# A fused graph, attention and mixture layer: short edge rows, and a written order for the first tokens, weights and products

## The chip, the cores and the metric

The kernel runs on one core of one Trainium2 chip. Its time is the device time in microseconds (us) of one execution; shown is the median of three runs.

## What is computed

One layer of a graph transformer on 625 tokens of 1024 features, all float32. `src` and `dst` hold 20,000 edges, sorted by `dst`.

```python
xn = _layernorm(x)
x = x + gnn(xn, src, dst) + mix(xn)       # both read the same normalised tokens
x = x + ffn(_layernorm(x))
# gnn: two layers h @ W_self + mean @ W_neigh + b, relu between them;
#      mean = segment_sum(h[src], dst) / max(degree, 1)
# mix: q, k, v products, softmax of q over features and of k over tokens,
#      context = k^T v, attn = q context, product with Wo, plus bo
# ffn: softmax router, the best 2 of 8 experts silu(x w1) w2, and a gated shared expert
```

## The kernel before

Every float32 product is made of three TensorE products: each operand is split into a rounded `hi` and the rest `lo`, and `hi*hi + hi*lo + lo*hi` is summed in PSUM. `split` (L93, its instructions stand at L94) makes the pair: ScalarE casts `hi`, and VectorE (or GpSimd, by `eng`) subtracts to get `lo`. Weights come in blocks of 128 x 1024 through `Stream`: `load` issues the transfer on SP's queue (`wraw`, three buffers), `next` splits it into `whi` and `wlo`.

The start of the kernel, which the change touches, runs so:

- `load_x` reads the tokens in five tiles of 128 rows (`xts`); `src` and `dst` come as 10 rows of 2000 (`ei`). All of it is issued on SP: tiles 0 and 1, the edges, the first weight block, tiles 2 to 4.
- `first_stats` and `first_norm` compute mean and inverse deviation (`inv_std`, seven small VectorE instructions and one square root on ScalarE) and normalise. Tiles 0 and 1 are done in one batch, tiles 2 to 4 in another; even tiles are scaled on VectorE (L328), odd ones on ScalarE (L326). `first_turn` transposes a tile on TensorE (`pst`, L276) and splits it into `xnh` and `xnl`.
- The edges are cast to float32 (`edges`, L334), turned by 32 small transposes (`psed`, L338) and one more (`psf`, L343), and copied to `edt` and `first_dst`.
- `keys_step` makes the products of the keys (`psk`, L398 to L400) and then of the self term of the graph layer. There are 64 steps of 12 matmuls; a weight block `o` has two column parts of two steps each. The first three blocks do their columns 0 to 255 first (steps 0 to 5, which need only token tiles 0 and 1), then columns 256 to 625 (steps 6 to 11). `keys_exp` takes a maximum on VectorE (L376) and the exponential on ScalarE (L378), `keys_back` transposes the result (`pskt`, L370). A block `o` is split at a step of block `o-1`; the `lo` parts of blocks 0 to 8 are made on GpSimd (L94 POOL), later ones on VectorE.
- The adjacency is counted by TensorE from one-hot rows: 160 chunks of 125 edges. `one_hots` makes a chunk's pair on VectorE (L454, L455) in a ring `hot` of 40 places, after eight GpSimd instructions (L436 to L446) have prepared `edt`, `srow` and `unit`; `count_chunks` multiplies the pair (`pa`, L477) and adds 16 chunks at a time to `packed` (L481). 36 pairs are made ahead; then each step of the loop makes 4 pairs and counts 4.

A scheduler orders the instructions of an engine by priority and by its own estimates. `keep` (`tc.keep_in_program_order`) pins an instruction behind the one traced before it on its engine, `tc.issue_after` behind a named one, and `tc.high_priority` ranks a block first. [...]After the key stage come queries, values, graph aggregation and experts, on which nothing is changed.

## Time and profile before

| what | value |
|---|---|
| median of 3 runs | 1057.1 us (1052.38 to 1058.31) |
| profiled execution | 1056.29 us, span 1054.3 us |
| mean granted TensorE clock | 0.983 |
| TensorE matmul busy (PE) | 1010.2 us, 96% |
| VectorE busy (DVE) | 601.1 us, 57% |
| ScalarE busy (ACT) | 394.9 us, 37% |
| GpSimd busy (POOL) | 175.0 us, 17% |
| read from and written to memory | 133.06 MB and 30.16 MB, 155 GB/s over the span |

Busy shares are averages over the whole span. PEld is TensorE loading weights beside its matmuls; SPq is the queue on which SP issues transfers. Matmuls overlap, so that the start-to-start distance of two of them, not the duration of one, is their price in a stream. In an answer about waits, a row has the waiting engine with its tile and line, what it waited for, and the total, the number and the longest of the waits. In a timeline, a row has its start, its duration, the engine, the line, the operation, and what the tile is written from.

### The profile page before, as it was taken

Reading aid. Unit: us, or ns where it says so; the run is one execution under the profiler, and the core shown is the slowest. Engines: PE = TensorE matmul, PEld = TensorE weight load, DVE = VectorE, ACT = ScalarE, POOL = GpSimd, SP = SyncE. Lnnn points to the kernel's source line nnn. Section 1 sums busy time; section 2 is a strip of 40 time slices with the busy share of each in tenths; the row PEclk is TensorE's granted clock in tenths of the full one; section 3 lists DMA queues with packets and bytes.
Section 4 is the critical chain, followed back from the end, with each engine's and each line's share of the span. In section 5 each row is a group of like instructions: output and inputs, shape, how many; then the busy total and the mean of one; then the engine's idle time right before and its main releaser. Section 6 shows DMA issues by size and latency. Waiting matters only on the chain. (4 is left out here: it accounts for less than half of the span.)

```text
span 1054.3 us, 14764 instructions
## 1 busy us (share of the span) xinstructions
PE 1010.2 (96%) x5571; PEld 870.8 (83%) x5571; DVE 601.1 (57%) x1190; ACT 394.9 (37%) x577; POOL 175.0 (17%) x206
## 2 busy tenths in 40 slices
PE   6889999999999999999999999999999899999958
PEld 4889998888878888988877999997888688787746
DVE  3899941672343334533337364288776878878632
ACT  3333432232131122222115242175755676677200
POOL 2421002110044100200001004023111213300500
PEclk7999999999999999999999999999999999999979
DMA  6121226665235422322220127477788899879812
GB/s 183 42 80 52 70 81 205 223 217 175 81 110 172 134 76 66 111 72 76 80 81 2 44 78 250 140 221 217 247 261 236 281 306 284 272 256 308 313 50 82
DMA packets 117792, 164.33 MB, mean 156 GB/s; under 512 B 12533, under 2 KB 69885, under 8 KB 117710
## 3 DMA queue, kind: packets, MB, share of 16 engines
q1 hardware_dynamic: 97774, 118.54, 35.9%
q0 software_dynamic: 19936, 44.74, 13.0%
q8 instruction: 47, 0.77, 0.3%
q14 instruction: 35, 0.29, 0.1%
HBM read 133.06 MB, written 30.16 MB: 155 GB/s over the span
## 5 line engine op out<-in xcount | busy, mean ns | idle before, releaser
L94 DVE TENSOR_TENSOR wlo<-wraw,whi 128x1024 fp32r<-128x1024 f32 x140 | 178.7, 1276 | 257.6 <-ACT whi L94 256.5
L94 ACT CAST whi<-wraw 128x1024 fp32r<-128x1024 f32 x149 | 156.4, 1051 | 291.4 <-PE psg L205 66.2
L1120 PE MATMUL pse<-xs,whi 128*128 128x448 f32 (+1 forms) x384 | 109.2, 357 | 0.0
L94 DVE TENSOR_TENSOR wlo<-wmore,whi 128x1024 fp32r<-128x1024 f32 x67 | 86.9, 1297 | 26.3 <-ACT whi L94 25.3
L94 ACT CAST whi<-wmore 128x1024 fp32r<-128x1024 f32 x67 | 70.3, 1049 | 64.3 <-PE psz L205 33.3
L1116 PE MATMUL pse<-xs,wlo 128*128 128x224 f32 (+1 forms) x384 | 90.1, 255 | 0.7 <-DVE wlo L94 0.6
L398 PE MATMUL psk<-xnh,whi 128*128 128x314 f32 (+3 forms) x256 | 82.7, 324 | 0.6 <-ACT xnh L94 0.6
L399 PE MATMUL psk<-xnl,whi 128*128 128x314 f32 (+3 forms) x256 | 79.5, 311 | 1.1 <-DVE xnl L94 1.1
L400 PE MATMUL psk<-xnh,wlo 128*128 128x314 f32 (+3 forms) x256 | 79.5, 311 | 0.0
L1116 PEld LDWEIGHTS pse<-xs,wlo 128*128 128x128 f32 x384 | 72.0, 190 | 2.9 <-DVE wlo L94 2.0
L1172 PE MATMUL psy<-wlo,he 128*128 128x512 f32 (+1 forms) x176 | 69.9, 397 | 3.3 <-DVE wlo L94 2.9
L1120 PEld LDWEIGHTS pse<-xs,whi 128*128 128x128 f32 x384 | 69.0, 189 | 2.4
L1171 PE MATMUL psy<-whi,he 128*128 128x512 f32 (+1 forms) x176 | 69.4, 395 | 0.0
L1173 PE MATMUL psy<-whi,he 128*128 128x512 f32 (+1 forms) x176 | 69.1, 392 | 0.0
L455 DVE TENSOR_SCALAR hot<-iota,srow,unit 125x128 f16<-125x128 f16 x160 | 55.3, 346 | 0.0
L399 PEld LDWEIGHTS psk<-xnl,whi 128*128 128x128 f32 x256 | 49.5, 193 | 1.4 <-DVE xnl L94 1.4
L94 POOL TENSOR_TENSOR xs<-raw,xs 128x512 fp32r<-128x512 f32 (+2 forms) x24 | 34.3, 1452 | 96.7 <-ACT xs L94 75.2
L398 PEld LDWEIGHTS psk<-xnh,whi 128*128 128x128 f32 x256 | 49.3, 193 | 1.1 <-ACT xnh L94 1.1
L400 PEld LDWEIGHTS psk<-xnh,wlo 128*128 128x128 f32 x256 | 49.1, 192 | 0.2 <-POOL wlo L94 0.2
L454 DVE TENSOR_SCALAR hot<-iota,edt 125x128 f16<-125x128 f16 x160 | 45.7, 286 | 1.7 <-POOL edt L444 1.7
L203 PE MATMUL psz<-whi,sth 128*128 128x512 f32 (+1 forms) x80 | 32.1, 401 | 14.4 <-DVE x L1249 12.9
L1172 PEld LDWEIGHTS psy<-wlo,he 128*128 128x128 f32 (+1 forms) x176 | 31.8, 180 | 14.9 <-DVE wlo L94 6.7
(340 smaller groups left out, 2375.1 us busy)
## 6 DMA issues: line engine op xcount, KB each, us to landing
wraw<-in_L_ffn_w_dram SPq DMA_DIRECT2D x65, 512.0 KB, 5.5
wmore<-in_L_ffn_w_dram SPq DMA_DIRECT2D x63, 512.0 KB, 5.2
xsd<-zt POOLq DMA_DIRECT2D x9, 1024.0 KB, 5.6
wraw<-in_L_gnn_W_self_dram SPq DMA_DIRECT2D x16, 512.0 KB, 3.8
wraw<-in_L_gnn_W_neigh_dram SPq DMA_DIRECT2D x16, 512.0 KB, 3.7
wraw<-_ffn_shared_gate_up_dram SPq DMA_DIRECT2D x16, 512.0 KB, 3.8
wraw<-in_L_mix_Wk_dram SPq DMA_DIRECT2D x8, 512.0 KB, 4.2
wraw<-in_L_mix_Wq_dram SPq DMA_DIRECT2D x8, 512.0 KB, 3.7
```

Source lines behind the costliest of these rows:

```text
L94: return (nc.scalar.copy(hi, srcap), (eng or nc.vector).tensor_sub(lo, srcap, hi.bitcast(F32)))
L203: nc.tensor.matmul(acc, xh[:, kt, c], wh[:, k, :], start=f, stop=False)
L398: nc.tensor.matmul(ps[:, :n], wh[:, kt, :], xnh[:, kt, c], start=kt == 0, stop=False)
L399: nc.tensor.matmul(ps[:, :n], wh[:, kt, :], xnl[:, kt, c], start=False, stop=False)
L400: nc.tensor.matmul(ps[:, :n], wl[:, kt, :], xnh[:, kt, c], start=False, stop=kt == KT - 1)
L454: nc.vector.tensor_scalar(h[:ET, :WIN], iota[:ET, :WIN], edst[:, i, g:g + 1], None, op0=ALU.is_equal)
L455: nc.vector.tensor_scalar(h[:ET, WIN:], iota[:ET, :WIN], srow[:ET, i, g:g + 1], unit[:ET, i, g:g + 1].bitcast(F32), op0=ALU.is_equal, op1= ...
L1116: nc.tensor.matmul(ps[a][:, :n], wl[:, k, c], xs[:, kt, 0, :], start=False, stop=False)
L1120: nc.tensor.matmul(ps[a][:, :2 * n], wh[:, k, c], xs[:, kt], start=kt == 0, stop=kt == KT - 1)
L1171: nc.tensor.matmul(acc, h(kt, 0), wh[:, k, :], start=kt == 0, stop=False)
L1172: nc.tensor.matmul(acc, h(kt, 0), wl[:, k, :], start=False, stop=False)
L1173: nc.tensor.matmul(acc, h(kt, 1), wh[:, k, :], start=False, stop=kt == KT - 1)
```

## The change

- The edges are read as 80 rows of 250 (`EP`), issued on ScalarE's queue; `ei` and `edges` move to the pool `edgep`, and four transposes and one take the place of 33. `edt`, `field`, `srow` and `unit` get a new layout of the same size.
- The transfers of tokens 2 to 4 alternate with those of the first three weight blocks on SP.
- Statistics, scales, weight splits, transposes and the first products stand in one written sequence, tile by tile, and nearly all are pinned by `keep`. All five tiles are normalised on ScalarE. Two key steps stand between the transposes of tiles 1 and 2, of 2 and 3, and of 3 and 4, where before four and two stood before tiles 2 and 3.
- Only blocks 0 to 2 have their `lo` part made on GpSimd; blocks 3 to 8 move to VectorE.
- 40 one-hot pairs are made ahead; in the loop the four chunks are counted before new pairs are made, and three pairs a step are made while `ks[0]` is below 40, then four. The register load of a group's first column is queued behind the last pair made.

The diff, without the lines that only follow the new layout in the rarely taken `recount`:

```diff
...
 NG = 10
 ET = 125
 CH = E // (ET * NG)
+EP = E // (2 * ET)
 WIN = 128
 SPAN = NP + WIN
 BITS = 5
...
     def bank(name="ps"):
         return psum.tile([128, 512], F32, name=name, tag="ps")
-    def split(srcap, hi, lo, eng=None):
-        return (nc.scalar.copy(hi, srcap), (eng or nc.vector).tensor_sub(lo, srcap, hi.bitcast(F32)))
+    def split(srcap, hi, lo, eng=None, order=lambda ins: ins):
+        return (order(nc.scalar.copy(hi, srcap)), order((eng or nc.vector).tensor_sub(lo, srcap, hi.bitcast(F32))))
     class Stream:
...
                 self.raw[self.loaded] = r
                 self.loaded += 1
-        def next(self, eng=None):
+        def next(self, eng=None, **order):
             if self.ready:
                 return self.ready.pop(0)
             i = self.used
...
             else:
                 hi = wts.tile([128, D], F32R, name="whi", tag="whi")
                 lo = wts.tile([128, D], F32R, name="wlo", tag="wlo")
-            split(r, hi, lo, eng)
+            split(r, hi, lo, eng, **order)
             b = ap.shape[2]
             return (hi.rearrange("p (a b) -> p a b", b=b), lo.rearrange("p (a b) -> p a b", b=b))
...
         for h in range(2):
             if half is None:
                 order(nc.vector.bn_stats(st6[:mv.shape[0], h, :], xt[:, h * 512:(h + 1) * 512]))
-        nc.vector.bn_aggr(mv, st6[:mv.shape[0]])
-    def inv_std(var, y, z, a):
-        nc.vector.tensor_scalar(a, var, EPS, None, op0=ALU.add)
-        nc.scalar.activation(y, a, AF.Sqrt)
-        nc.vector.reciprocal(y, y)
-        nc.vector.tensor_mul(z, y, y)
-        nc.vector.tensor_mul(z, z, a)
-        nc.vector.tensor_scalar(z, z, -0.5, 1.5, op0=ALU.mult, op1=ALU.add)
-        nc.vector.tensor_mul(y, y, z)
+        (order or (lambda ins: ins))(nc.vector.bn_aggr(mv, st6[:mv.shape[0]]))
+    def inv_std(var, y, z, a, order=lambda ins: ins):
+        order(nc.vector.tensor_scalar(a, var, EPS, None, op0=ALU.add))
+        order(nc.scalar.activation(y, a, AF.Sqrt))
+        order(nc.vector.reciprocal(y, y))
+        order(nc.vector.tensor_mul(z, y, y))
+        order(nc.vector.tensor_mul(z, z, a))
+        order(nc.vector.tensor_scalar(z, z, -0.5, 1.5, op0=ALU.mult, op1=ALU.add))
+        order(nc.vector.tensor_mul(y, y, z))
     def normalise(eng, yt, xt, mean, y, z):
         if eng is nc.vector:
...
         return nat.rearrange("p (c k) -> p k c", k=KT)
-    def to_t(nat, t, hi, lo, order=None):
+    def to_t(nat, t, hi, lo, order=None, both={}):
         for g in range(2):
             ps = bank("pst").rearrange("p (a b) -> p a b", b=128)
             for k in range(4):
...
                 tr = nc.tensor.transpose(ps[:, k, rows(t)], nat[:, kt], ident[rows(t), rows(t)])
                 if order:
                     order(tr)
-            done = split(ps[:, :, rows(t)], hi[:, 4 * g:4 * g + 4, cols(t)], lo[:, 4 * g:4 * g + 4, cols(t)])
+            done = split(ps[:, :, rows(t)], hi[:, 4 * g:4 * g + 4, cols(t)], lo[:, 4 * g:4 * g + 4, cols(t)],
+                         **both)
         return done
     def pad(*tiles):
...
     xnh, xnl = slot_t("xnh"), slot_t("xnl")
     pad(xnh, xnl)
-    ei = big.tile([128, 2, CH * ET], I32, name="ei", tag="big")
+    ei = edgep.tile([EP, 2, 2 * ET], I32, name="ei")
     xts = big.tile([128, NT, D], F32, name="xts", tag="big")
     keep = tc.keep_in_program_order
...
         for r, p in pieces(t):
             keep(nc.sync.dma_start(xts[p, t, :], x[r, :]))
-    for t in range(2):
-        load_x(t)
+    load_x(0)
+    load_x(1)
     for i, e in enumerate((src, dst)):
-        keep(nc.sync.dma_start(ei[:NG, i, :], e.rearrange("(p c) -> p c", p=NG)))
-    st.load(1)
+        keep(nc.scalar.dma_start(ei[:, i, :], e.rearrange("(p c) -> p c", p=EP)))
     for t in range(2, NT):
+        st.load(t - 1)
         load_x(t)
     lnv = const.tile([128, NT, 2], F32, name="lnv")
...
     def first_stats(t):
         stats(xts[rows(t), t, :], lnv[rows(t), t, :], order=keep)
-    def first_norm(a, b):
-        inv_std(lnv[:T, a:b, 1], lnt[:T, 0, a:b], lnt[:T, 1, a:b], lnt[:T, 2, a:b])
-        y, z = lnt[:T, 0, :], lnt[:T, 1, :]
-        nc.vector.scalar_tensor_tensor(z[:, a:b], lnv[:T, a:b, 0], -1.0, y[:, a:b], op0=ALU.mult, op1=ALU.mult)
-        for t in range(a, b):
-            p = rows(t)
-            xt = xts[p, t, :]
-            if t % 2:
-                nc.scalar.activation(xt, xt, AF.Identity, bias=z[p, t:t + 1], scale=y[p, t:t + 1])
-            else:
-                nc.vector.tensor_scalar(xt, xt, lnv[p, t, 0:1], y[p, t:t + 1], op0=ALU.subtract, op1=ALU.mult)
-    def first_turn(t, order=None):
-        return to_t(xts[rows(t), t, :].rearrange("p (k c) -> p k c", c=128), t, xnh, xnl, order)
-    edges = big.tile([128, 2, CH * ET], F32, name="edges", tag="big")
-    nc.scalar.copy(edges[:NG], ei[:NG])
-    edt = edgep.tile([128, 2 * CH, NG], F32, name="edt")
-    pse = bank("psed")[:, :2 * CH * NG].rearrange("p (a b) -> p a b", b=NG)
-    for i in range(2 * CH):
-        nc.tensor.transpose(pse[:ET, i, :], edges[:NG, i // CH, (i % CH) * ET:(i % CH + 1) * ET], ident[:NG, :NG])
-    nc.scalar.copy(edt[:ET], pse[:ET])
-    esrc, edst = edt[:ET, :CH, :], edt[:ET, CH:, :]
-    psf = bank("psf")
-    nc.tensor.transpose(psf[:, :NG], edges[:NG, 1, 0:1].to_broadcast([NG, 128]), ident[:NG, :NG])
+    def first_scale(t):
+        inv_std(lnv[:T, t:t + 1, 1], *(lnt[:T, i, t:t + 1] for i in range(3)), order=keep)
+        keep(nc.vector.scalar_tensor_tensor(lnt[:T, 1, t:t + 1], lnv[:T, t:t + 1, 0], -1.0, lnt[:T, 0, t:t + 1],
+                                            op0=ALU.mult, op1=ALU.mult))
+    def first_norm(t):
+        p = rows(t)
+        keep(nc.scalar.activation(xts[p, t, :], xts[p, t, :], AF.Identity,
+                                  bias=lnt[p, 1, t:t + 1], scale=lnt[p, 0, t:t + 1]))
+    def first_turn(t):
+        return to_t(xts[rows(t), t, :].rearrange("p (k c) -> p k c", c=128), t, xnh, xnl, keep, dict(order=keep))
+    edges = edgep.tile([EP, 2, 2 * ET], F32, name="edges")
+    edt = edgep.tile([128, 2, 2, NG, CH // 2], F32, name="edt")
+    esrc, edst = edt[:ET, 0], edt[:ET, 1]
     first_dst = edgep.tile([128, NG], F32, name="first_dst")
-    nc.scalar.copy(first_dst, psf[:, :NG])
     first_col = edgep.tile([1, NG], I32, name="first_col")
-    with tc.high_priority():
-        for t in range(2):
-            first_stats(t)
-        first_norm(0, 2)
-        first_stats(2)
-        for t in range(2):
-            first_turn(t)
+    def turn_edges():
+        pse = bank("psed")[:, :4 * EP].rearrange("p (a b) -> p a b", b=EP)
+        for i in range(4):
+            nc.tensor.transpose(pse[:ET, i, :], edges[:, i // 2, (i % 2) * ET:(i % 2 + 1) * ET], ident[:EP, :EP])
+        keep(nc.scalar.copy(edt[:ET].rearrange("p a h g j -> p (a h) (g j)"), pse[:ET]))
+        psf = bank("psf")
+        nc.tensor.transpose(psf[:, :EP], edges[:, 1, 0:1].to_broadcast([EP, 128]), ident[:EP, :EP])
+        keep(nc.scalar.copy(first_dst, psf[:, :EP].rearrange("p (g j) -> p g j", g=NG)[:, :, 0]))
     shared = big.tile([128, 8 * NP], F32, name="shared", tag="big")
     kbuf = shared[:, 5 * NP:].rearrange("p (i s) -> p i s", s=NP)
...
         o, i, h = s // 4, s // 2 % 2, s % 2
         if s < 12:
             o, i = s // 2 % 3, s // 6
-        if s in (0, 2, 4):
-            wks[o] = st.next(nc.gpsimd)
         if (o, i, h) == (1, 1, 0):
-            wks[3] = st.next(nc.gpsimd)
+            wks[3] = st.next()
         if i == 0 and h == 0 and 2 < o < 2 * KT - 1:
-            wks[o + 1] = st.next(nc.gpsimd if o < KT else None)
+            wks[o + 1] = st.next()
         if h == 0:
             kps[0] = bank("psk")
         wh, wl = wks[o]
...
             if k < 8 * KT:
                 keys_step(k)
+    def keys_weights(o):
+        wks[o] = st.next(nc.gpsimd, order=keep)
     with tc.high_priority():
-        keys_steps(4)
+        first_stats(0)
+        first_scale(0)
+        first_norm(0)
+        keep(nc.scalar.copy(edges, ei))
+        first_stats(1)
+        first_scale(1)
+        keys_weights(0)
+        first_norm(1)
+        first_stats(2)
+        first_turn(0)
+        first_turn(1)
+        turn_edges()
+        keys_weights(1)
+        first_scale(2)
+        first_norm(2)
         first_stats(3)
+        first_scale(3)
+        keys_weights(2)
+        first_norm(3)
+        keys_steps(2)
+        first_turn(2)
         first_stats(4)
-        first_norm(2, NT)
-        first_turn(2, keep)
+        first_scale(4)
+        first_norm(4)
         keys_steps(2)
-        first_turn(3, keep)
-        last = first_turn(4, keep)
-    field = edgep.tile([128, CH, NG], F32, name="field")
-    srow = edgep.tile([128, CH, NG], F32, name="srow")
-    unit = edgep.tile([128, CH, NG], I32, name="unit")
+        first_turn(3)
+        keys_steps(2)
+        last = first_turn(4)
+    field = edgep.tile([128, 2, NG, CH // 2], F32, name="field")
+    srow = edgep.tile([128, 2, NG, CH // 2], F32, name="srow")
+    unit = edgep.tile([128, 2, NG, CH // 2], I32, name="unit")
     keep(nc.gpsimd.tensor_scalar(field[:ET], esrc, 1.0 / T, -0.496, op0=ALU.mult, op1=ALU.add))
     keep(nc.gpsimd.tensor_scalar(field[:ET], field[:ET], MAGIC, None, op0=ALU.add))
     keep(nc.gpsimd.tensor_scalar(field[:ET], field[:ET], MAGIC, None, op0=ALU.subtract))
...
     keep(nc.gpsimd.tensor_scalar(unit[:ET], field[:ET], BITS * 2.0 ** 23, (127.0 - 2 * BITS) * 2.0 ** 23,
                                  op0=ALU.mult, op1=ALU.add))
-    keep(nc.gpsimd.tensor_sub(edst, edst, first_dst[:ET, None, :].to_broadcast([ET, CH, NG])))
+    keep(nc.gpsimd.tensor_sub(edst, edst, first_dst[:ET, None, :, None].to_broadcast([ET, 2, NG, CH // 2])))
     keep(nc.gpsimd.tensor_copy(first_col, first_dst[:1]))
...
     nc.gpsimd.memset(packed, 0.0)
     def one_hot(h, i, g):
-        nc.vector.tensor_scalar(h[:ET, :WIN], iota[:ET, :WIN], edst[:, i, g:g + 1], None, op0=ALU.is_equal)
-        nc.vector.tensor_scalar(h[:ET, WIN:], iota[:ET, :WIN], srow[:ET, i, g:g + 1],
-                                unit[:ET, i, g:g + 1].bitcast(F32), op0=ALU.is_equal, op1=ALU.mult)
-    pa, made, counted = [None], [0], [0]
+        e = (slice(0, ET), i // 8, g, slice(i % 8, i % 8 + 1))
+        nc.vector.tensor_scalar(h[:ET, :WIN], iota[:ET, :WIN], edst[e], None, op0=ALU.is_equal)
+        return nc.vector.tensor_scalar(h[:ET, WIN:], iota[:ET, :WIN], srow[e], unit[e].bitcast(F32),
+                                       op0=ALU.is_equal, op1=ALU.mult)
+    pa, made, counted, hots = [None], [0], [0], []
     def one_hots(n):
         for _ in range(n):
             c = made[0]
             if c < NG * CH:
                 made[0] += 1
-                one_hot(hot[:, c % RING, :], c % CH, c // CH)
+                hots.append(one_hot(hot[:, c % RING, :], c % CH, c // CH))
     def count_chunks(n):
         for _ in range(n):
...
             h = hot[:ET, c % RING, :]
             nc.tensor.matmul(pa[0][:, :WIN], h[:, WIN:], h[:, :WIN], start=i == 0, stop=i == CH - 1)
             if i == CH - 1:
-                first_v = nc.vector.value_load(first_col[0:1, g:g + 1], min_val=0, max_val=N - 1)
+                with tc.issue_after(hots[-1].ins):
+                    first_v = nc.vector.value_load(first_col[0:1, g:g + 1], min_val=0, max_val=N - 1)
                 to = packed[:T, ds(first_v, WIN)]
                 nc.vector.tensor_add(to, to, pa[0][:T, :WIN])
...
     nc.tensor.transpose(psb[:, :KT], b0n, ident[:KT, :KT])
     nc.vector.tensor_copy(b0t, psb[:, :KT])
     with tc.issue_after(last[0].ins), tc.issue_after(last[1].ins):
-        one_hots(RING - 4)
+        one_hots(RING)
     knat = slot_n("knat")
     hself = slot_t("hself", F32)
     while ks[0] < 8 * KT:
         keys_steps(1)
-        one_hots(4)
         count_chunks(4)
+        one_hots(3 if ks[0] < 5 * KT else 4)
     ath = atp.tile([128, NT, XP], F32R, name="ath")
...
```

More of the change, by code (lines that the diff above doesn't have):

```diff
@@ L557, in recount @@
         ct = tmp.tile([128, HW], F32, name="ct", tag="tmp")
-        nc.vector.tensor_tensor(edst, edst, first_dst[:ET, None, :].to_broadcast([ET, CH, NG]), op=ALU.add)
+        nc.vector.tensor_tensor(edst, edst, first_dst[:ET, None, :, None].to_broadcast([ET, 2, NG, CH // 2]), op=ALU.add)
         nc.vector.tensor_scalar(field[:ET], esrc, float(HW), None, op0=ALU.is_ge)
@@ L567, in recount @@
                     h = tmp.tile([128, WIN + HW + 1], F16, name="hrare", tag="tmp")
-                    nc.vector.tensor_scalar(h[:ET, :WIN], iota[:ET, :WIN], edst[:, i, ds(g, 1)], None, op0=ALU.is_equal)
-                    nc.vector.tensor_scalar(h[:ET, WIN:WIN + HW], iota[:ET, :HW], esrc[:, i, ds(g, 1)],
-                                            field[:ET, i, ds(g, 1)], op0=ALU.is_equal, op1=ALU.mult)
+                    nc.vector.tensor_scalar(h[:ET, :WIN], iota[:ET, :WIN], edst[:, i // 8, ds(g, 1), i % 8], None, op0=ALU.is_equal)
+                    nc.vector.tensor_scalar(h[:ET, WIN:WIN + HW], iota[:ET, :HW], esrc[:, i // 8, ds(g, 1), i % 8],
+                                            field[:ET, i // 8, ds(g, 1), i % 8], op0=ALU.is_equal, op1=ALU.mult)
                     nc.tensor.matmul(ps[:, :HW], h[:ET, :WIN], h[:ET, WIN:WIN + HW], start=i == 0, stop=i == CH - 1)
```

## The prediction

> **What bounds the kernel now.** The page comes first: TensorE.
>
> ```profile
> PE 1010.2 (96%) x5571; PEld 870.8 (83%) x5571; DVE 601.1 (57%) x1190; ACT 394.9 (37%) x577; POOL 175.0 (17%) x206
> ...
> PE   6889999999999999999999999999999899999958
> ...
> PEclk7999999999999999999999999999999999999979
> ```
>
> PE is full but for the first three slices (26.4 us each) and the last two. Which idle times those are, PE's answer about waits says, over the whole run:
>
> ```profile
> PE psz L203 <- DVE x L1249: 12.9, 1, 12.9
> PE psed L338 <- ACT edges L334: 7.9, 1, 7.9
> PE pskt L370 <- ACT shared L378: 3.0, 1, 3.0
> ...
> PE pst L276 <- DVE xts L328: 2.0, 1, 2.0
> ```
>
> The 12.9 us lie at 1012, behind a gather that the change leaves alone; the others lie in the first 68 us. The timeline of that stretch:
>
> ```profile
> 11.57 3.51 ACT L334 CAST edges<-ei 10x4000 f32<-10x4000 int32 x1
> ...
> 15.23 6.86 PE L338 MATMUL psed<-ident,edges 10*125 10x10 f32 x32 [7.85 <-ACT edges L334]
> ...
> 22.12 3.28 PE L276 MATMUL pst<-ident,xts 128*128 128x128 f32 x16
> ...
> 25.62 0.38 PE L398 MATMUL psk<-xnh,whi 128*128 128x256 f32 x1 [0.22 <-ACT xnh L94]
> ...
> 34.48 1.38 PE L276 MATMUL pst<-ident,xts 128*128 128x128 f32 x8 [2.04 <-DVE xts L328]
> ...
> 43.72 0.44 PE L399 MATMUL psk<-xnl,whi 128*128 128x370 f32 x1 [0.79 <-DVE xnl L94]
> ```
>
> Tokens 0 and 1 are scaled by 11.7, but PE turns them at 22.12, behind the edges; the first product is at 25.62. PE waits for the scaling of tile 2, and the wide steps run from 43.7. The clock in windows of 2 us (the last three columns are granted clock, DMA share, GB/s):
>
> ```profile
> 32.00:34.00 2.00, 0.44 (x4) 0.24 (x2) 1.67 (x7) 0.47 (x2) 1.75 (x4) 1.00 0.61 182
> ...
> 36.00:38.00 2.00, 2.00 (x11) 2.00 (x10) 1.27 (x5) 0.49 (x1) 0.82 (x3) 0.50 0.02 7
> ```
>
> After a gap of 2.04 us the clock halves. Last, the timeline at the later stall of 3.0 us:
>
> ```profile
> 55.99 4.81 POOL L94 TENSOR_TENSOR wlo<-wraw,whi 128x1024 fp32r<-128x1024 f32 x2 [4.65 <-ACT whi L94]
> ...
> 56.11 2.39 DVE L455 TENSOR_SCALAR hot<-iota,srow,unit 125x128 f16<-125x128 f16 x1
> ...
> 58.42 2.43 DVE L454 TENSOR_SCALAR hot<-iota,edt 125x128 f16<-125x128 f16 x1
> ...
> 65.25 0.78 DVE L376 TENSOR_REDUCE mx<-shared 128x1 f32<-128x625 f32 x1
> ...
> 67.31 0.77 PE L370 MATMUL pskt<-ident,shared 128*128 128x128 f32 x5 [2.98 <-ACT shared L378]
> ```
>
> A one-hot of 0.3 us takes 2.4 while GpSimd subtracts a weight; the maximum L376 stands behind some 40 pairs on DVE, its exponential behind that, and PE behind both.
>
> **The change part by part.** PE is full from 68 us to 1012 and its work there is the same, so the sum is the shift of the transposes L370 that start at 67.31.
>
> *Edges.* The cast of 4000 numbers a row took 3.51 us, 0.88 ns each; 500 make 0.44, and with the 0.17 us of the smallest ACT instructions 0.6. 33 transposes end 6.9 us after the first starts, 0.21 each at half clock; five make 1.1. Transfers: the same 156 KB as 160 rows of 1000 bytes instead of 20 of 8000. SP loses two issues (0.41 and 0.30 us), ScalarE gains them at about 2.5 us, where it is idle until 9.0. The landing of short rows is not shown: between no later than before and 2 us later. I take 0, as the cast waits for `first_norm(0)` at 9.1 anyway; later than that, ScalarE is held with tile 1 behind it.
>
> *Transfers in turn.* SP's order is tokens 0, 1, weight 0, token 2, weight 1, token 3, weight 2, token 4. The bytes are the same (4.2 MB), and in the trace they have landed by about 17.3 us (DMA share 1.15 at 16 to 17, then 0.34). Token 2 stays near 12.3, token 4 moves from about 16 to 17.3. Nothing below needs it before 27. Weight 0 is not timed, only bounded: after token 1 (7.2), before token 2 (12.3). I take 11; at 12.3 all that follows comes 1.2 later.
>
> *Normalising tile by tile.* DVE loses three scalings (0.81 us) and gains three more chains of seven small instructions, 1.4 us each by 8.80 to 10.39; ScalarE gains three of 1.24 us and three roots of 0.2. So I lay the written order out by hand. Tile 0: statistics 4.65 to 6.2, scale 7.8, normalised 9.1, turned on PE by 10.9. Edge cast to 9.6. Tile 1: statistics from 7.85, scale 11.0. ScalarE then has weight 0 (1.05) to 12.05 and tile 1 to 13.3; PE turns it by 15.0; four casts (0.55) to 15.6, DVE's subtractions (0.65) behind the statistics of tile 2 to 16.5. PE turns the edges beside that, and the first product starts at 16.0 instead of 25.62. Steps 0 and 1 (24 matmuls at 0.213 cold, 0.118 warm) end at about 20.
>
> *Behind it.* ScalarE: the two edge copies (0.6), weight 1 to 17.55, root of tile 2. GpSimd's `lo` of weight 1 lasts from 17.6 to 20.0, and the chain of tile 2 has TENSOR_SCALARs; in the trace such a one took 2.12 us beside GpSimd (L252). So tile 2 is normalised at 20.5 to 21.75; tile 3, behind its statistics (1.5), chain and weight 2, at 24.8. The casts of tile 2 (behind tile 3's norm) end at 26.3, its subtractions at 27.0; only then come statistics and chain of tile 4 (1.5 and 2.3, with some 1 us of collisions with the eight GpSimd edge instructions), scaled at 30.8 to 32.05. ScalarE still has casts and key copies of tiles 3 and 4, to 34.9. Step 6 starts at about 34.5 where it did at 41.99.
>
> PE has by then steps 2 to 5 (11.4 us at most), turned tiles 2 and 3, and two gaps, about 2.9 and 1.5 us. Here a rule bears: the Trainium skill, "TensorE: Matmul & The Clock Gate", section "HAM oscillation", asks for no idle gap above about 3.4 us. By that rule these gaps cost nothing further. The row above speaks against it: 2.04 us sufficed, and 3.4 us then ran at half clock. I follow the trace: half of 3.4, 1.7 us. Step 6 starts in effect at 36.2, against 43.3 before (the end of step 11 at 55.55, less 72 matmuls of 0.17). That is 7.1 us.
>
> *The stall L370.* The `lo` parts of blocks 3 to 8 leave GpSimd: six of 2.4 us, each of which held a DVE instruction as long; DVE pays 1.23 us instead (L94 DVE). The Trainium skill, "SBUF — State Buffer", section "Who interferes with whom", speaks against moving them: a DVE instruction with two SBUF inputs contends with a GpSimd one that reads SBUF. But GpSimd has nothing else there, so by rule and trace the price is 1.23. From the last subtraction (35.6) DVE needs 40 pairs at 0.385 (start to start), a maximum 0.93, one `lo` 1.28, the second maximum 0.93, the exponential 1.1: ready at 55.2. PE arrives at 36.2 + 12.3 + 0.5 + four steps of 2.03 = 57.1. No stall: 3.0 us more, with 1.9 to spare. Shift in all 10.1.
>
> *Three pairs a step.* Per block of four steps (8.6 us on PE) DVE has 12 pairs 4.6, `lo` 1.28, maximum 0.93, an addition 0.25: 7.1. The lead shrinks from 40 to about 10 chunks at the 27th step and stays there. Cost 0 while DVE keeps its 1.5 us a block; without that cover PE waits at L477. The register loads (10) and the moved `ei` and `edges` (buffers of `big` come free earlier) have no row: 0, bounded by -0.5 and +1.
>
> Sum: the profiled 1056.29 (span 1054.3 and 2.0 around it) less 10.1 is 1046.2. The median shown is 0.8 above that execution, so I say 1046.
>
> **The rivals.**
> *A smoother start.* The scheduler puts unpinned steps 2 to 5 into the gaps, the clock stays warm, the port is free: step 6 at about 33, the shift then limited by DVE's 55.2 to some 12 to 14 us: 1043. For it: 41 to 44 has three gaps below 0.9 us and a full clock. Against: tile 4's chain ends late whatever PE does.
> *A head of the line.* Everything on ScalarE is pinned; a weight landing 3 us late holds the token behind it. Each such wait passes to tile 4; two cost 5 to 6: 1051. For: 512-byte rows of the weights, three transfers ahead of token 4. Against: all have landed by 17.3.
> *Slower: one-hots become the bound.* With three pairs a step and all `lo` parts on DVE, PE waits at L477 in each block. It decides from a DVE block of 8.6 us, that is pairs of 0.51 us; at the 0.63 us that the page's means of L454 and L455 add up to, a block takes 10.0 and ten blocks lose 14, so 1060. Against: these means hold overlap and port waits, and the start-to-start distance is 0.385.
> *It does not do what it says:* PE's unpinned steps or the edge transposes are ordered as before; then about 3 us remain, 1053.
>
> **How the numbers follow.** Below 0.5% (5.3 us) the measurement cannot tell a gain from no change. Hand sum 0.62 (1046, 1043 to 1049), smoother 0.16, head of the line 0.12 (half of it within 0.5%), order as before 0.06, slower 0.04. Faster 0.85, same 0.11, slower 0.04. The range 1040 to 1052 leaves out the slow case, most of "as before", and the ends of the others.
>
> **What would show it.** Five edge transposes instead of 33; first L398 near 16 (right: below 18); the first step over 370 columns near 34.5, preceded by two gaps and a clock of 0.5; no wait of `pskt` above 1 us; DVE `lo` parts of 1.2 us from block 3 on and no one-hot of 2.4; no wait of L477 for `hot`. I am wrong if the wide steps start after 39, or if PE waits in the key stage for `hot` or `wlo`.

## The result, and the profile after

The changed kernel takes 1041.44 us (median of four runs, 1040.14 to 1043.89), against 1056.19 for the kernel before (four runs, 1052.38 to 1058.31). The ratio is 0.9867, with a 95% interval of 0.9832 to 0.9902. The profiled executions stand at 1041.64 us (span 1039.9) and 1056.29 (span 1054.3).

The page after, in the lines that were shown of before: busy times, TensorE in 40 slices, granted clock.

```profile
PE 1004.7 (97%) x5543; PEld 865.0 (83%) x5543; DVE 594.3 (57%) x1214; ACT 396.7 (38%) x583; POOL 159.0 (15%) x200
...
PE   7999999999999999999999999999999999999878
...
PEclk8999999999999999999999999999999999999989
```

TensorE's work is the same but for 28 small transposes; only the first slices are fuller. What it waits for in the first 170 us, by the answer about waits:

```profile
PE pst L277 <- ACT xts L327: 6.9, 4, 2.2
PE pswarm L240 <- DVE cold L237: 1.5, 1, 1.5
PE pskt L364 <- ACT shared L372: 0.6, 1, 0.6
PE psk L390 <- ACT xnh L95: 0.2, 1, 0.2
```

The 7.9 us for the edges are gone, and 3.0 of `pskt` have become 0.6. In their place stand four waits for tiles that ScalarE has yet to scale (L327). TensorE's timeline, cut to what carries the reading:

```profile
9.42 1.06 PE L277 MATMUL pst<-ident,xts 128*128 128x128 f32 x8 [2.18 <-ACT xts L327]
12.37 1.97 PE L277 MATMUL pst<-ident,xts 128*128 128x128 f32 x8 [1.89 <-ACT xts L327]
14.13 0.97 PE L343 MATMUL psed<-ident,edges 80*125 80x80 f32 x4
...
14.97 0.56 PE L390 MATMUL psk<-xnh,whi 128*128 128x256 f32 x1
...
21.17 1.10 PE L277 MATMUL pst<-ident,xts 128*128 128x128 f32 x8 [1.87 <-ACT xts L327]
...
29.85 0.99 PE L277 MATMUL pst<-ident,xts 113*128 113x113 f32 x8 [0.97 <-ACT xts L327]
31.09 0.78 PE L390 MATMUL psk<-xnh,whi 128*128 128x370 f32 x3 [0.24 <-ACT xnh L95]
...
43.78 0.71 PE L364 MATMUL pskt<-ident,shared 128*128 128x128 f32 x5
```

Three landmarks say where the time came from. The wide steps start at 31.09 instead of 41.99. The first transposes L364, which close them, start at 43.78 instead of 55.55: 11.8 us. The second start at 53.12 instead of 67.31: 14.2 us. At the first query product it is still 14.2 (150.74 for 164.92). From there to the end the two profiles take 889.2 and 889.4 us; in all the profiles below this stretch lies between 886.8 and 892.8, so that the close agreement of these two is partly luck. The spans differ by 14.4.

The chain that now sets the start is on VectorE and ScalarE. VectorE's timeline has one long instruction in it, beside GpSimd's subtraction of weight 1:

```profile
16.66 2.40 POOL L95 TENSOR_TENSOR wlo<-wraw,whi 128x1024 fp32r<-128x1024 f32 x1 [3.39 <-ACT whi L95]
```

```profile
16.91 2.16 DVE L256 TENSOR_TENSOR lnt<-lnt 128x1 f32<-128x1 f32 x1
19.10 0.16 DVE L257 TENSOR_TENSOR lnt<-lnt 128x1 f32<-128x1 f32 x1
```

A product of two columns of one number each takes 2.16 us, where the next one takes 0.16. It ends with GpSimd's subtraction (19.07 and 19.06), and all of tile 2 waits behind it.

### The profile page after: what moved, and what is told of

It is laid out like the page before. It is cut to its first block, busy times and chain, and to the rows that moved or that the text cites. A ratio compares the mean times of both kernels' runs of the same rounds, so it can differ in the third digit from the quotient of the medians.

```text
span 1039.9 us, 14735 instructions
## 1 busy us (share of the span) xinstructions
PE 1004.7 (97%) x5543; PEld 865.0 (83%) x5543; DVE 594.3 (57%) x1214; ACT 396.7 (38%) x583; POOL 159.0 (15%) x200
## 5 line engine op out<-in xcount | busy, mean ns | idle before, releaser
L95 DVE TENSOR_TENSOR wlo<-wraw,whi 128x1024 fp32r<-128x1024 f32 x146 | 185.5, 1270 | 262.1 <-ACT whi L95 258.2
```

Source lines behind the costliest of these rows:

```text
L95: return (order(nc.scalar.copy(hi, srcap)), order((eng or nc.vector).tensor_sub(lo, srcap, hi.bitcast(F32))))
```

## The experiments

For each run three things are compared: the time, the start of the first transposes L364 (55.55 before; 43.78 changed), which measures the first stage, and the start of the first query product (164.9 before; 150.7 changed), where the key stage is over. The landmarks leave out what happens at the end of the kernel, where a gather scatters by some microseconds from run to run. Ratios are to runs of the kernel before on the same chip, and differ clearly only where their intervals part. A landmark comes from one profiled execution; the two of the changed kernel lie 1.1 us apart at both landmarks, so a difference of that size says nothing. "Later" below is against the changed kernel's first profile.

| run | ratio and interval | first L364 | first query product |
|---|---|---|---|
| edges alone | 0.9927 (0.9905 to 0.9949) | 47.24 | 159.7 |
| long edge rows | 0.9932 (0.9910 to 0.9954) | 52.40 | 159.4 |
| lo parts on GpSimd | 0.9918 (0.9891 to 0.9945) | 45.09 | 158.1 |
| key copies pinned | 0.9903 (0.9870 to 0.9936) | 46.93 | 153.9 |
| no pins | 0.9873 (0.9850 to 0.9896) | 46.75 | 153.7 |
| one-hots as before | 0.9861 (0.9834 to 0.9888) | 49.23 | 155.4 |
| tokens first | 0.9853 (0.9826 to 0.9881) | 46.53 | 153.5 |
| scale first, 12 pairs in the loop | 0.9896 (0.9870 to 0.9922) | 50.25 | 156.4 |
| scale first | 0.9831 (0.9808 to 0.9854) | 42.59 | 149.5 |
| gaps filled | 0.9867 (0.9846 to 0.9888) | 43.63 | 150.6 |
| changed kernel again | 0.9845 (0.9824 to 0.9866) | 44.85 | 151.8 |
| scale first, filled, ring of 36 | 0.9807 (0.9779 to 0.9836) | 42.78 | 149.0 |

### The edges alone

The kernel before, with the edges read as 80 short rows, turned by five transposes and laid out as in the change; the rest untouched.

```diff
-        keep(nc.sync.dma_start(ei[:NG, i, :], e.rearrange("(p c) -> p c", p=NG)))
+        keep(nc.scalar.dma_start(ei[:, i, :], e.rearrange("(p c) -> p c", p=EP)))
...
-    for i in range(2 * CH):
-        nc.tensor.transpose(pse[:ET, i, :], edges[:NG, i // CH, (i % CH) * ET:(i % CH + 1) * ET], ident[:NG, :NG])
+    for i in range(4):
+        nc.tensor.transpose(pse[:ET, i, :], edges[:, i // 2, (i % 2) * ET:(i % 2 + 1) * ET], ident[:EP, :EP])
```

> The kernel before with the edges alone changed: 80 short rows issued on ScalarE's queue, five transposes, the new layout; order, weights and one-hots as before. Theory A (the gain is made of three separate parts; the order of ScalarE and VectorE sets where the wide steps start): the transposes of tiles 0 and 1 move from 22.1 to about 15, the first product from 25.6 to about 18 to 19, but tile 2 is still scaled in one batch with tiles 3 and 4, so the wide steps start only 4 to 7 us earlier, and the wait of pskt stays near 3 us: 1050 to 1052. Rival B (short edge rows carry the whole change): wide steps near 32 and 1042 to 1044. Rival C (the edges were off the path): 1056.

1048.74 us, a little better than theory A's 1050 to 1052. Tiles 0 and 1 are turned at 14.07, the wide steps start at 34.48, 7.5 us earlier: more than expected. But 3.0 of the 8.3 us at the first transposes (L371 here) are lost again by the queries. TensorE's waits and windows of this run (each row ends with the granted clock, the DMA share and GB/s):

```profile
PE pskt L371 <- ACT shared L379: 3.4, 1, 3.4
```

```profile
58.00:62.00 4.00, 2.58 (x11) 2.58 (x12) 4.00 (x17) 2.97 (x6) 1.30 (x1) 0.54 0.00 0
62.00:66.00 4.00, 4.00 (x22) 3.81 (x21) 4.00 (x14) 0.00 (x0) 1.15 (x1) 0.60 0.39 116
```

TensorE comes earlier and waits longer for the maximum and exponential behind VectorE's queue (3.4 us for 3.0), and half clock follows this wait. In the changed kernel, where blocks 3 to 8 no longer stand in VectorE's way, the same edges keep what they bring, as the next run shows.

The rest of the change takes the wide steps from 34.48 to 31.09. The written order itself, tile by tile instead of in two batches, was not undone in any run, so its own part in these 3.4 us is not shown.

### The edges undone

```diff
-    ei = edgep.tile([EP, 2, 2 * ET], I32, name="ei")
+    ei = big.tile([128, 2, CH * ET], I32, name="ei", tag="big")[:NG]
...
-        keep(nc.scalar.dma_start(ei[:, i, :], e.rearrange("(p c) -> p c", p=EP)))
+        keep(nc.sync.dma_start(ei[:, i, :], e.rearrange("(p c) -> p c", p=NG)))
```

and the 33 transposes and the old layout with it.

> The changed kernel with the edges as before: 10 rows of 2000 issued on SP behind token tile 1, a cast of 3.5 us, 32 transposes and one; all else as changed, so the cast stands on ScalarE between tile 0 and tile 1. Theory A: ScalarE is held 2.9 us longer ahead of tile 1, and PE 5.8 us longer ahead of the first product; the first product goes from 15.0 to about 23 to 24, the wide steps from 31.5 to about 37 to 39: 1047 to 1049. Rival B (short rows carry everything): 1054 or more. Rival C (the written order hides the edges): within 2 us of 1041.

1049.42 us, just above the expected 1047 to 1049. The cast of 10 rows holds ScalarE from 8.87 to 12.38 with tile 1 behind it, and TensorE turns edges for 6.89 us at half clock before the first product at 23.8; wide steps at 39.70. With ten columns a transpose TensorE counted as busy, and yet its clock did not come up: it is 0.50 in every window from 14 to 26. By difference the short rows are worth 8.6 us in the changed kernel, at the first L364 and at the queries alike, and alone 5.3 at the queries.

### The lo parts back on GpSimd

```diff
-            wks[3] = st.next()
+            wks[3] = st.next(nc.gpsimd)
...
-            wks[o + 1] = st.next()
+            wks[o + 1] = st.next(nc.gpsimd if o < KT else None)
```

> The changed kernel with the lo parts of blocks 3 to 8 made on GpSimd again. Theory A: the wide steps start at 31.5 as in the changed kernel, GpSimd holds VectorE for three times 2.4 us before the second maximum, less the 1.2 us of the block that VectorE no longer makes; the second pskt waits 4 to 7 us instead of 0.6: 1045 to 1048. Rival D (the stall before came from the order of VectorE's queue, not from GpSimd): pskt waits below 1 us, 1041.

1048.17 us, just above theory A's 1045 to 1048. The stall is back, and larger, and with it the one-hots that GpSimd holds; TensorE's wait, and one of them on VectorE's timeline:

```profile
PE pskt L364 <- ACT shared L372: 4.0, 1, 4.0
```

```profile
44.55 2.56 DVE L472 TENSOR_SCALAR hot<-iota,srow,unit 125x128 f16<-125x128 f16 x1
```

The third L364 comes 11.3 us after the second instead of 8.7, since half clock follows this wait too (0.50 at 58 to 62). At the queries 7.4 us are lost, 1.3 of them before the first L364: there the clock fell after a gap of 2.75 us ahead of tile 2, before GpSimd had any of the blocks put back. The lo parts themselves are thus worth about 6. The second maximum stands behind 80 one-hot instructions here, in the changed kernel and in the kernel before, so the rival that blamed the order of VectorE's queue falls.

### The key copies pinned

```diff
-                nc.scalar.copy(kbuf[:, o % 3, c0:c0 + n], ps[:, :n])
+                (keep if s < 6 else lambda ins: ins)(nc.scalar.copy(kbuf[:, o % 3, c0:c0 + n], ps[:, :n]))
```

In the changed kernel ScalarE cast the first half of tile 2 at 22.55, ahead of the scaling of tile 3 at 23.03. Its timeline:

```profile
21.02 0.35 ACT L396 COPY shared<-psk 128x256 f32<-128x256 f32 x1
...
22.55 0.58 ACT L95 CAST xnh<-pst 128x512 fp32r<-128x512 f32 x1
23.03 1.25 ACT L327 ACTIVATE xts<-xts,lnt 128x1024 f32<-128x1024 f32 x1
```

The source has them the other way round, and both are pinned. But a pin holds an instruction behind the one traced just before it, and that was the key copy of step 1, which is not pinned: it went ahead (21.02), and with it the end of the chain of pins.

> The changed kernel with the three key copies among steps 0 to 5 pinned as well, so that ScalarE casts tile 2 behind the scaling of tile 3, and tile 3 behind that of tile 4, as the prediction assumed. Theory A (the prediction's 3 us too late were this order): wide steps at 33 to 35 instead of 31.5, and two gaps on TensorE of which one is above 2 us; 1043 to 1046. Rival E (the order of these casts is hidden by VectorE): wide steps within 0.5 us of 31.5, 1041. On the clock: if a gap above 2 us halves it, 1.7 us come on top.

1045.30 us: in theory A's range, but not by its way. With the copies pinned ScalarE does follow the source, and yet the wide steps start at 31.65, only 0.6 later, as rival E said. (Here tile 1 was turned at full clock, which brought tile 2 forward by 0.9, so the order itself is worth about 1.5, by difference.) The larger loss at the landmark is the clock:

```profile
29.70 0.99 PE L277 MATMUL pst<-ident,xts 113*128 113x113 f32 x8 [1.66 <-ACT xts L327]
31.65 1.29 PE L390 MATMUL psk<-xnh,whi 128*128 128x370 f32 x3 [0.95 <-ACT xnh L95]
```

```profile
32.00:34.00 2.00, 2.00 (x7) 1.56 (x7) 1.07 (x5) 0.03 (x1) 0.00 (x0) 0.50 0.00 0
34.00:36.00 2.00, 2.00 (x8) 2.00 (x7) 2.00 (x12) 0.00 (x0) 0.00 (x0) 0.50 0.00 0
36.00:38.00 2.00, 2.00 (x9) 2.00 (x9) 2.00 (x11) 0.00 (x0) 0.00 (x0) 0.60 0.00 0
```

Gaps of 1.66 and 0.95 us with 1 us of transposes between them were followed by half clock for some 6 us of the wide steps: 46.93 instead of 43.78 at the first L364. This is one execution; the ratio's interval overlaps that of the changed kernel.

### No pins

Statistics, scales, weights, transposes and edge copies written as in the change, without `keep`.

> The changed kernel with the sequence written as it is but nothing in it pinned (statistics, scales, weights, transposes and edge copies left to the scheduler's priorities); transfers pinned as before. Theory A (the order itself, tile by tile, is what counts, and priorities keep most of it): wide steps at 31 to 35, 1041 to 1046. Rival F (only the pins make the order): the edges or the statistics run ahead, wide steps after 37, 1047 or more.

1044.63 us; wide steps at 34.06. The scheduler kept nearly all of the order. What it moved is at the head of ScalarE's queue:

```profile
6.85 0.61 ACT L425 CAST edges<-ei 80x500 f32<-80x500 int32 x1 [4.38 <-DMA ei<-in_dst_dram]
7.36 0.20 ACT L254 ACTIVATE lnt<-lnt 128x1 f32<-128x1 f32 x1
8.87 1.04 ACT L95 CAST whi<-wraw 128x1024 fp32r<-128x1024 f32 x1 [1.30 <-DMA wraw<-in_L_mix_Wk_dram]
9.82 1.24 ACT L330 ACTIVATE xts<-xts,lnt 128x1024 f32<-128x1024 f32 x1
```

The root of tile 0 waits behind edges that land at 6.8, and its scaling behind weight 0, which lands at 8.8: tile 0 is scaled at 9.82 instead of 8.04. In this profile the first of these transposes (L367 here) is 3.0 us later; by the times the two kernels can't be told apart.

### The one-hots undone

```diff
-        one_hots(RING)
+        one_hots(RING - 4)
...
-        count_chunks(4)
-        one_hots(3 if ks[0] < 5 * KT else 4)
+        one_hots(4)
+        count_chunks(4)
```

> The changed kernel with the one-hots as before: 36 pairs ahead, four pairs in each step ahead of the counting. Theory A (three pairs a step cost and bring nothing of their own; VectorE has cover): the second maximum stands behind 36 pairs and none of the loop's first four or behind 40 as before, the wait of pskt stays at 0.6 or up to 1, and later ones stay away: 1041 to 1043. Rival G (three pairs a step give VectorE the time for the lo parts of blocks 4 to 8): with 16 pairs a block VectorE needs 8.6 us a block, as much as TensorE, so pskt or the first product of a block waits in several blocks: 1044 to 1048.

1044.09 us, above theory A's range and at the lower end of rival G's, but by a way that neither had. VectorE's timeline, and TensorE's after it:

```profile
25.13 1.27 DVE L249 BATCH_NORM_STATS2 bnst<-xts 113x6 f32<-113x512 f32 x2
28.92 0.25 DVE L471 TENSOR_SCALAR hot<-iota,edt 125x128 f16<-125x128 f16 x1 [2.52 <-POOL edt L460]
29.09 0.20 DVE L250 BATCH_NORM_AGGREGATE lnv<-bnst 113x2 f32<-113x12 f32 x1
```

```profile
32.53 1.08 PE L277 MATMUL pst<-ident,xts 113*128 113x113 f32 x8 [3.91 <-ACT xts L327]
```

A one-hot stands between the statistics of tile 4 and their aggregate, and waits 2.52 us for GpSimd. VectorE took its queue in order: the statistics end at 26.4, the aggregate starts at 29.09. `issue_after` holds the 36 pairs of the block behind the last subtraction; the first pairs of the loop are not in the block, and four places of the ring are free, so the scheduler let them go ahead. With 40 pinned pairs there is no free place. Tile 4 is 2.7 us late, half clock follows its gap of 3.9 us, and the first L364 is at 49.23, 5.4 us later. After it no product waited for VectorE, in this run or with three pairs a step. The profile is of the slowest of four executions (1047.14, the others 1040.91 to 1044.10), and by the ratios this kernel can't be told from the changed one: the trace shows the way, and the 5.4 us are of this execution. The kernel before shows the same wait in VectorE's timeline, ahead of the subtraction of tile 2 at 37.51:

```profile
36.73 0.26 DVE L454 TENSOR_SCALAR hot<-iota,edt 125x128 f16<-125x128 f16 x1 [1.66 <-POOL edt L444]
```

### Tokens first

```diff
+    st.load(1)
     for t in range(2, NT):
-        st.load(t - 1)
         load_x(t)
+    st.load(3)
```

> The changed kernel with the transfers in the order of before: weight 0 ahead of tokens 2 to 4, weights 1 and 2 behind them. Theory A (all bytes have landed by 18 us and nothing waits for a transfer after token 0): weight 1 lands at 17 instead of before 15.5 and holds ScalarE, whose queue has it ahead of tile 2, by about 1.5 us; wide steps at 32 to 34: 1041 to 1044. Rival H (transfers in turn are the gain): wide steps after 35, 1046.

1043.27 us, in theory A's range, but not by its way. ScalarE waited 0.72 us for weight 1, which landed at 15.48; its cast began no later than in the changed kernel (15.52). Nothing waited for weight 2. The first of these transposes (L365 here) is 2.8 us later. In this run the clock stood at half from about 14 to 28 us; the steps ended late and held ScalarE's key copies, ahead of tile 2's scaling and again at 28.50. Whether the order of the transfers has a part in that isn't shown; by the times it makes no difference that can be measured.

### Scale first, with 12 pairs in the loop

The chain of tile 2 written ahead of weight 1, to be over before GpSimd subtracts it; and 12 of the 40 pairs moved into the loop's first step.

```diff
-        keys_weights(1)
         first_scale(2)
+        keys_weights(1)
...
-        one_hots(RING)
+        one_hots(RING - 12)
...
-        one_hots(3 if ks[0] < 5 * KT else 4)
+        one_hots((3 if ks[0] < 5 * KT else 4) + (12 if counted[0] == 4 else 0))
```

> The changed kernel with two changes of order: the scale of tile 2 is written ahead of weight 1, so that its chain on VectorE is over before GpSimd subtracts weight 1, and 12 of the 40 pairs made ahead are made in the loop's first step, behind the second maximum. Theory A (tile 2's chain, held 2.2 us by GpSimd, sets all that follows; the second maximum stands behind 40 pairs): tile 2 is turned at about 19 instead of 21.2, wide steps at 29 to 30, pskt does not wait: 1038.5 to 1039.5, that is 2 to 3 us less than the changed kernel. Rival I (the transfers or ScalarE's own work set tile 4): wide steps stay at 31, and 0.6 us is all: 1041.

1045.94 us: both theories failed. Twelve pairs were now free to go ahead of tile 4, and did: the first waited 2.51 us for GpSimd and stands at 27.94, ahead of the aggregate of tile 4 at 28.10. TensorE waited 3.7 us for its scaling, and the wide steps started at 33.2 at half clock. (Tile 2 was turned at 19.76, near what theory A said.)

### Scale first alone

> The changed kernel with the scale of tile 2 written ahead of weight 1 and nothing else (all 40 pairs stay pinned behind the last subtraction). Theory A (in the run with 12 pairs in the loop, pairs that were not pinned went ahead of tile 4's chain and cost 3 to 4 us; without them the earlier tile 2 is a gain): tile 2 turned at 19.5 to 20, no hot ahead of tile 4, wide steps at 29 to 30.5, 1038.5 to 1040.5. Rival I (tile 4 is set by something else): wide steps at 31, 1041. Rival J (the clock, not the order, decides: an earlier tile 2 only makes a longer gap elsewhere): wide steps at 30 at half clock, 1042 to 1043.

1039.00 us, as theory A said: tile 2 turned at 19.80, wide steps at 29.90 at full clock, first L364 at 42.59, 1.2 us before the changed kernel's first profile and 2.3 before its second. No pair goes ahead of tile 4, which fits the reading of the run with 12 pairs in the loop and of the one with the one-hots undone. The interval of its ratio overlaps that of the changed kernel, so that a gain in the time is not shown.

### The gaps filled, and the changed kernel again

Matmuls on a zero tile in the gaps, their result not used: 29 instead of 20 at the start, 7 between tiles 0 and 1, 7 behind step 1, 4 behind step 5.

```diff
+    def fill(n):
+        ps = bank("psfill")
+        for i in range(n):
+            keep(nc.tensor.matmul(ps, cold[:, :128], cold, start=i == 0, stop=i == n - 1))
```

> The changed kernel with matmuls on a zero tile in TensorE's gaps: 29 instead of 20 at the start, 7 between the transposes of tiles 0 and 1, 7 behind step 1, 4 behind step 5; their result is not used. Theory K (the clock halves after gaps of 1 to 3 us, at a point that differs from run to run, and that is most of the scatter of these kernels): clock 1.0 from 6 to 40 us, first product still at 15, step 1 over at 18, wide steps at 31; not faster in the profile than the changed kernel's, but the runs lie closer, 1039.5 to 1041. Rival L (the clock is the same in every run of a kernel, and fillers only take time): 1041 to 1043 with the same scatter, wide steps later by up to 1 us.

> The changed kernel once more, unchanged. Theory K: its profile shows the half clock in other windows than the first profile (11.4 to 17.7 there), and its wide steps or the transposes behind step 11 shift by 0 to 4 us with it; times between 1040 and 1045. Rival L: the same windows within 0.5 us, transposes behind step 11 at 43.8.

The changed kernel's second profile is 1.1 us later at the first L364. The clock made that, in the same program. First its windows from 18 to 24, then those of the first profile:

```profile
18.00:20.00 2.00, 0.29 (x3) 0.09 (x1) 1.86 (x6) 0.22 (x1) 0.96 (x1) 1.00 0.00 0
20.00:22.00 2.00, 0.93 (x9) 0.93 (x9) 1.63 (x6) 1.87 (x4) 0.00 (x0) 1.00 0.87 261
22.00:24.00 2.00, 2.00 (x13) 2.00 (x12) 1.33 (x6) 2.00 (x3) 1.38 (x1) 0.60 0.05 9
```

```profile
18.00:20.00 2.00, 1.30 (x11) 1.09 (x10) 1.86 (x6) 0.12 (x1) 1.05 (x1) 1.00 0.00 0
20.00:22.00 2.00, 0.83 (x8) 0.83 (x9) 1.63 (x6) 1.87 (x4) 0.00 (x0) 1.00 0.84 248
22.00:24.00 2.00, 2.00 (x19) 2.00 (x18) 1.42 (x6) 2.00 (x3) 1.28 (x1) 1.00 0.08 22
```

In the second the clock came up two microseconds earlier (full at 16 to 18, 0.56 in the first), so steps 0 and 1 were over sooner, the gap ahead of tile 2 grew from 1.87 to 2.79 us, and the clock fell again. Filled, it is 1.00 in every window from 4 to 44 us; tile 2 is turned at 20.20, but the wide steps start at 30.94, much as in the first profile. So theory K is right that the clock differs from run to run, and wrong on the scatter: the filled runs lie between 1039.84 and 1045.53, with a median of 1041.85. Of the 4.4 us between the spans of the changed kernel's two profiles 1.1 are there at the queries, and 2.6 come from VectorE's last wait for the gather, first profile first:

```profile
1007.91 1.41 DVE L1266 SCALAR_TENSOR_TENSOR x<-ys,top,x 113x512 f32<-113x512 f32 x2 [1.43 <-DMA ys<-ysd,slot]
```

```profile
1012.07 1.41 DVE L1266 SCALAR_TENSOR_TENSOR x<-ys,top,x 113x512 f32<-113x512 f32 x2 [4.07 <-DMA ys<-ysd,slot]
```

### The best version

Scale first; a ring of 36, all pinned; fillers 26, 6 and 3.

> The changed kernel with the scale of tile 2 ahead of weight 1, a ring of 36 pairs of which all 36 are made ahead and pinned, and matmuls on a zero tile in TensorE's gaps (26 at the start, 6 between tiles 0 and 1, 3 behind step 5). Theory A: with a full clock steps 0 and 1 end at 18, tile 2 is turned at 18.2 and tile 4 by 28.5, the wide steps start at 28.5 to 29.5, the second pskt does not wait; the transposes behind step 11 at 41 to 41.5 (43.8 and 44.9 in the two profiles of the changed kernel, 42.6 with the scale alone), the first query product at 147.5 to 148.5 (150.7 and 151.8): 1037.5 to 1039.5. Rival I (tile 4 is set by ScalarE's work): transposes behind step 11 at 42.5 and 1039 to 1040.5.

1040.20 us on a chip where the kernel before took 1060.47: a ratio of 0.9807 (0.9779 to 0.9836), below both of the changed kernel (their intervals reach 0.9832 and 0.9824 at the low end, so they overlap, and a gain is not shown). Steps 0 and 1 end by 18, tile 2 is turned at 18.07, and `pskt` no longer waits. But the wide steps start at 30.09, and the first L364 is at 42.78, no better than with the scale alone. The numbers are rival I's, yet ScalarE is not the cause: it waited 2.04 us for VectorE ahead of the scaling of tile 3. GpSimd's timeline, then VectorE's:

```profile
19.62 2.40 POOL L95 TENSOR_TENSOR wlo<-wraw,whi 128x1024 fp32r<-128x1024 f32 x1 [0.62 <-ACT whi L95]
```

```profile
19.63 2.40 DVE L322 SCALAR_TENSOR_TENSOR lnt<-lnv,lnt 128x1 f32<-128x1 f32 x1
```

The last instruction of tile 3's chain started 0.01 us after GpSimd's subtraction of weight 2 and was held for all of it. The wait was moved from tile 2 to tile 3.

This is decided by hundredths of a microsecond. In the changed kernel the same instruction of tile 3 started at 22.71, 0.01 us before the subtraction, and took 0.16; with the scale alone at 21.52 against 21.53, and took 0.16 too. Other executions of these kernels may fall either way; no run shows how often.

## Why the prediction was right, and where its sum was off

The time lies in the range (1040 to 1052), 4.6 us below the forecast of 1046. What was to be gained and why is right: the edges out of TensorE's way, an earlier tile 2 to 4, and the stall gone with GpSimd's blocks. The sum gave 10.1 us where the profiled executions differ by 14.65: 4.7 more before the first L364 (11.8 for 7.1), 0.6 less at the stall, and the rest behind the key stage. The large misses point the same way, and it is the width of the range that holds the result. By its own rule (0.8 above the profiled execution) the sum gives 1047, not 1046.

- *First product.* Forecast 16.0, measured 14.97. Weight 0 was taken to land at 11; the run without pins shows it at 8.8, and its cast came at 9.79, in time that ScalarE had free. Edges as forecast: cast 0.59 us for 0.6, five transposes 1.1 for 1.1.
- *The chain of tile 2.* The block by GpSimd came as forecast (2.16 us), but on the TENSOR_TENSOR at 16.91, where the working named a TENSOR_SCALAR. The rule that the prediction cites from the Trainium skill ("SBUF — State Buffer", section "Who interferes with whom") on two SBUF inputs covers this one, and the time agrees with it.
- *Wide steps: mis-sized.* Forecast 34.5, measured 31.09. Of these 3.4 us weight 0 left 0.6 at the scaling of tile 2 (19.88 for 20.5). About 1.5 came from "casts of tile 2 (behind tile 3's norm)": the source order was read as the queue's, and the unpinned key copy breaks the chain. The 1 us of collisions with GpSimd's edge instructions measured 0.04 (L259, 0.20 instead of 0.16). The 1.5 is by difference from the run with pinned copies; the other two are read from the trace, and no run parts them.
- *Clock: mis-sized.* "I follow the trace: half of 3.4, 1.7 us" measured 0, as the gaps ahead of the wide steps were 0.97 and 0.24 where the working had 2.9 and 1.5. Against the rule of 3.4 us from the Trainium skill ("TensorE: Matmul & The Clock Gate", section "HAM oscillation") the trace was nevertheless the better guide: gaps of 2.75 and 2.79 us were followed by half clock in two runs, and 1.66 and 0.95 together in a third. But one of 2.42 (one-hots as before) was not, so that length alone does not settle it.
- *The stall L370.* Forecast 3.0 us, measured 2.4. The cause was right (GpSimd's blocks, shown by putting them back). VectorE's side was ready at 53.1 where the working had 55.2; TensorE was there at 52.6 and not at 57.1, so that 0.6 remained instead of 1.9 to spare.
- *"Cost 0" for the one-hots: the 40 pairs had no line.* Three pairs a step cost nothing, as said (the lead falls to 13 chunks, not about 10). But pinned pairs that fill the ring keep unpinned ones from going ahead of tile 4, and that part of the change had no line in the sum. Undone, it cost 5.4 us at the first L364 in the one profile (2.7 of order, 2.7 of clock); by the times its worth is not shown.
- *Rivals.* The smoother start has the nearest time (1043) and its full clock came true from 18 us on, but not its mechanism: no step filled a gap, TensorE kept the written order. The head of the line occurs without pins (1.3 us for weight 0). One-hots never became the bound.

The edges, the lo parts and the one-hots, undone one at a time, cost 8.6, 7.4 and 4.7 us at the queries, 20.7 together, where the whole change brings 14.2. They don't add up, in part because those of the lo parts and of the one-hots have 1.3 and 2.7 us of half clock in them, which differs from run to run. In the times only the loss by the edges is clear of both runs of the changed kernel, and that by the lo parts of the second.

## What to carry to other kernels

When TensorE starts late, write down the order of the other engines' queues from the trace, not from the source: a pin holds only to the instruction traced before it, and unpinned work for which a buffer place is free can be put ahead of the critical chain, even when it then has to wait. Size a change by undoing each part in the finished kernel and by doing it alone, as a gain upstream can run into the next wait. Here a vector instruction of 0.16 us that started beside a GpSimd subtraction took up to 2.4, so put such chains where GpSimd is idle, and look again after moving them. Take the size of a part from times, not from one profile.

## What the runs showed of the hardware

- The length of a gap alone did not settle whether TensorE's clock halved: after 1.87 and 2.42 us the clock stayed full, after 2.04 (before, at 32), 2.75 and 2.79 it fell to half, after the wait of 2.98 us at 64 in the kernel before it stayed full, and after 3.4 and 3.98 it fell. The same program showed half clock in other windows from one profile to the next (11 to 17.7 us in the first, 12 to 15.5 and 22.4 to 25.8 in the second).
- Transposes of 10 columns left the clock at half for 6.9 us while TensorE counted as busy; in the kernel before and in the run with long rows alike.
- VectorE instructions of one to three numbers a row that started during a GpSimd subtraction lasted until its end, 2.1 to 2.4 us, in three forms: TENSOR_SCALAR (before, L252), TENSOR_TENSOR (L256) and SCALAR_TENSOR_TENSOR (best version, L322). One that started 0.01 us before it took 0.16. BATCH_NORM_STATS2 was not held (1.28 us at 10.96 in the changed kernel, during the subtraction of 10.90; 1.28 at 19.76 without one), and neither was a TENSOR_TENSOR with one operand in PSUM (0.69 at 23.16 during that of 22.72; 0.69 at 15.00 without).
